# Heads' stage of a spectral attention kernel: (key, head) chunks, one transfer for each repeated block, head weights written once

## The chip, the cores and the metric

The kernel runs on one core of one Trainium2 chip. The metric is the device time of one execution in microseconds (us), taken as the median of several runs. TensorE is called PE here, its weight load PEld, VectorE DVE, ScalarE ACT, GpSimd POOL and SyncE SP. SP computes nothing in this kernel; it issues most of the DMA transfers, and ACT issues some.

## What is computed

The input is (4, 48, 48, 128). Two layers follow each other, each as x = x + layer(group norm of x).

- Layer 0 is a state-space scan in four directions over 2304 positions, with a depthwise convolution ahead of it and a gate after it. The change does not touch it.
- Layer 1 takes each image as 48 tokens (the index that the kernel calls t), each a 48 x 128 field. Keys, queries and values of 32 heads are spectral convolutions of the normalized field. Attention between tokens is computed per head, the heads' outputs are projected by another spectral convolution, and two more spectral layers follow.

The core of layer 1 in the reference:

```
scores = einsum('bhtd,bhsd->bhts', q, k) / sqrt(d)
attn_w = softmax(scores, axis=-1)
out    = einsum('bhts,bhsd->bhtd', attn_w, v)
projd  = fno_layer(out over the 32 heads, wP, wPs, bPs)
```

In the Fourier domain, value and projection weights act mode by mode, so the kernel multiplies them together beforehand. What remains in the heads' stage is a sum over heads h and keys s, for each image b and each mode n:

```
z[b, t, n] = sum over h, s of  attn[b, h, t, s] * G[h, n] * X[b, s, n]
```

G are the head weights (complex, 1536 modes) and X is the spectrum of the tokens. The complex product is formed from three real ones: real parts, imaginary parts, and the sums of both.

## The kernel before

The program is one long list of instructions for five engines. Layer 0 fixes its order by hand. The part of layer 1 up to the end of the heads' stage does not: there a planner orders the instructions of each engine when the program is built, by when operands and buffers come free, and it puts in the waits. Each engine then runs its own list strictly in order. This holds for SP and ACT as issuers of transfers too: an issue whose buffer is still in use holds up all the issues behind it. `dmas` is the pair SP queue, ACT queue; the other transfers here are on SP.

**Head weights (L750 to L794).** The product G is formed in gw as 12 blocks of 128 modes. For each of four blocks k of 384 modes, PE transposes it to [32 heads, 3 x 384] (pgt), ACT copies it to gtt, and SP writes it to the scratch tensor dgt in HBM. dgt has an axis of 16 between the head and the modes: each head's row is written 16 times over, so that a later load of 8 heads fills 128 partitions from 128 rows.

**The stretch after it (L950 to L1030).** `spectral_weights` makes 16 blocks of weights for the later layers: POOL multiplies (wih), PE multiplies (psw, with three PSUM buffers in its pool), ACT copies to spw (L979, one buffer), SP writes spw to sp_d (L980). Beside it stand the group norm of xa, the first instance norm (`first_norm`: pm_in, then pv_in on PE, result in_r), and the forward transform along the width (`forward_w`: pa_x on PE, a_x on DVE, written to da_x), whose result comes back transposed as a2. The loads of the query and key weights (w_wQ, w_wK, many small transfers) are on SP's queue too.

**Scores (L1085 to L1170).** For each of two pairs of images the scores (sc) of all heads are accumulated on PE. DVE and ACT compute the softmax for eight heads at a time: maximum, exponential, sum, and the product sn with the reciprocal sum. Three transposes (pat) put 128 rows on the partitions: a chunk is one group g of 8 heads and one group q of 16 keys, and row 16 * head + key of it is one (head, key). ACT copies the result to attn_c. Beside this, `keys` writes the token spectrum to the scratch tensor dxt, rows of 3 x 384 numbers per token.

**Ahead of the heads' loop (L1190 to L1220).** wpv takes the products of two weight vectors per head, spread over the rows of a chunk; mask marks for each row which key it is. Both come in by eight small transfers per tensor, one for each run of 16 partitions. DVE forms e_w from them, and PE multiplies it with attn_c (pa, 48 matmuls for each pair), which ACT copies to a0_bd.

**The heads' loop (L1221 to L1275).** It runs over 2 pairs x 4 blocks of modes (8 blocks). One block takes three groups q of 16 keys and four groups g of 8 heads, 12 units:

- x (xrep, two buffers) holds, for both images, the 16 keys of group q repeated for 8 heads, on 128 partitions. It comes in as 8 transfers per image.
- r (grep, four buffers) holds the head weights of group g, each head repeated for 16 keys. It is loaded at q = 0 and kept for the block.
- ACT copies two thirds of r to gp in PSUM (two buffers); DVE multiplies gp with x into v; POOL multiplies the last third of r with x into v3. Both results have two buffers.
- PE contracts v and v3 with attn_c into acc, three PSUM banks with one buffer each, over the 12 units.

At the end of a block ACT copies the first bank to s1, DVE combines the three into zt (three instructions), PE transposes zt twice (pz), and ACT copies each to z2.

Of the kernel before, what the change touches and what calls it, by code (L numbers as in the profile page):

```python
# [10 lines left out]
F32 = mybir.dt.float32  # L11
# [8 lines left out]
B, T, H, W = 4, 48, 48, 128  # L20
# [9 lines left out]
NH = 32  # L30
# [613 lines left out]
def layer1(ctx, tc, io, x1_dram, out):  # L644
# [5 lines left out]
    nc = tc.nc  # L650
# [3 lines left out]
    dram = ctx.enter_context(tc.tile_pool(name="l1_dram", bufs=1, space=DRAM))  # L654
    dmas = [nc.sync, nc.scalar]
# [9 lines left out]
    ident = load("ident1", [128, 128], io["c_ident"])  # L665
# [84 lines left out]
    ws_p = everywhere("ws_p", io["wPs"].rearrange("o h -> (o h)"), NH)  # L750

    NC = 384
    dgt = dram.tile([4, NH, 16, 3 * NC], F32, name="dgt")
    with ExitStack() as pw:
        ps_t = pw.enter_context(tc.tile_pool(name="l1_wt", bufs=2, space=PSUM))
        q1 = pw.enter_context(tc.tile_pool(name="l1_w1", bufs=1))

        w_p = q1.tile([128, 12, 2, NH], F32, name="w_p")
        w_v = q1.tile([128, 6, 2, NH], F32, name="w_v")
        d48 = [q1.tile([128, 128], F32, name=f"d48{c}") for c in range(2)]  # L760
        for c in range(2):
            dmas[c].dma_start(w_p[:, :, c], io["wP"][c].rearrange("(j p) h -> p j h", p=128))
            dmas[c].dma_start(w_v[:, :, c], io["wV"][c].rearrange("(j p) h -> p j h", p=128))
            dmas[c].dma_start(d48[c], io[("c_D48r", "c_D48i")[c]])
        for c in range(2):
            p = ps_t.tile([128, 512], F32, tag="tr", name=f"pv48{c}")
            nc.tensor.matmul(p[:, 0:NH], d48[c], w_v[:, 0, c], start=True, stop=True)
            nc.scalar.copy(w_v[:, 0, c], p[:, 0:NH])
        gw = q1.tile([128, 12, 3, NH], F32, name="gw")
        for c in range(2):  # L770
            nc.vector.tensor_mul(gw[:, :, c], w_p[:, :, c], ws_v[:, None, :].to_broadcast([128, 12, NH]))
        half = [128, 6, NH]
        for c in range(2):
            g6 = gw[:, 0:6, c]
            t1 = q1.tile(half, F32, tag="gt", name=f"gt{c}_0")
            nc.vector.tensor_mul(t1, w_v[:, :, c], ws_p[:, None, :].to_broadcast(half))
            nc.vector.tensor_add(g6, g6, t1)
            for i in range(2):

                t2 = q1.tile(half, F32, tag="gt", name=f"gt{c}_{i + 1}")  # L780
                nc.vector.tensor_mul(t2, w_p[:, 0:6, i], w_v[:, :, (c + i) % 2])
                (nc.vector.tensor_sub if c == 0 and i == 1 else nc.vector.tensor_add)(g6, g6, t2)
        nc.vector.tensor_add(gw[:, :, 2], gw[:, :, 0], gw[:, :, 1])

        for k in range(4):
            gt = q1.tile([NH, 3, NC], F32, name=f"gtt{k}")
            for c in range(3):
                p = ps_t.tile([128, 512], F32, tag="tr", name=f"pgt{k}_{c}")
                for j in range(3):
                    nc.tensor.transpose(p[0:NH, j * 128 : (j + 1) * 128], gw[:, 3 * k + j, c], ident)  # L790
                nc.scalar.copy(gt[:, c], p[0:NH, 0:NC])
            nc.sync.dma_start(
                dgt[k], gt.rearrange("h c n -> h (c n)")[:, None].to_broadcast([NH, 16, 3 * NC])
            )  # L794
    ws_q = everywhere("ws_q", io["wQs"].rearrange("h o -> (h o)"), NH)
    ws_k = everywhere("ws_k", io["wKs"].rearrange("h o -> (h o)"), NH)
    a0_bd = const.tile([96, 2, 96], F32, name="a0_bd")
# [6 lines left out]
    dxt = dram.tile([B, 4, T, 3 * NC], F32, name="dxt")  # L804
# [272 lines left out]
    with ExitStack() as ph:  # L1077
# [33 lines left out]
        for pair in range(2):  # L1111
            sc = ps_1.tile([128, 4, 512], F32, tag="sc", name=f"sc{pair}")
            for jn in range(12):
                j, n = divmod(jn, 3)
                shape = [128, NH, T]
                on_pool = jn % 3 == 2
                f = []
                for b in range(2):
                    f.append(pf.tile(shape, F32, tag="f", name=f"f{pair}_{jn}_{b}"))
                    (nc.gpsimd if on_pool else nc.vector).tensor_mul(  # L1120
                        f[b],
                        (g_qk if on_pool else gp)[:, n, j, :, None].to_broadcast(shape),
                        ks[:, j, n, 2 * pair + b, None].to_broadcast(shape),
                    )
                for g in range(4):
                    for b in range(2):
                        nc.tensor.matmul(  # L1127
                            sc[64 * b : 64 * b + 64, g, 0 : 8 * T],
                            qs[:, j, n, 2 * pair + b],
                            f[b][:, 8 * g : 8 * g + 8],  # L1130
                            start=(jn == 0),
                            stop=False,
                        )
                for _ in range(2 - jn % 2 if pair == 0 else 1 + jn % 2):
                    next(beside, None)
            for g in range(4):
                for b in range(2):
                    nc.tensor.matmul(
                        sc[64 * b : 64 * b + T, g, 0 : 8 * T],
                        s0[:, 2 * pair + b],  # L1140
                        d_qk[:, 8 * g : 8 * g + 8],
                        start=False,
                        stop=True,
                    )
            for g in range(4):
                t = f"{pair}_{g}"
                v = sc[:, g, 0 : 8 * T].rearrange("p (h s) -> p h s", s=T)
                shape = [128, 8, T]
                mx = p2.tile([128, 8], F32, tag="mx", name=f"mx{t}")
                nc.vector.tensor_reduce(mx, v, AX.X, ALU.max)  # L1150
                s = p2.tile(shape, F32, tag="s", name=f"s{t}")
                nc.vector.tensor_sub(s, v, mx[:, :, None].to_broadcast(shape))
                nc.scalar.activation(s, s, AF.Exp, scale=scale)
                sm = p2.tile([128, 8], F32, tag="sm", name=f"sm{t}")
                nc.vector.tensor_reduce(sm, s, AX.X, ALU.add)
                nc.vector.reciprocal(sm, sm)
                sn = p2.tile([128, 3, 8, 16], F32, tag="sn", name=f"sn{t}")
                nc.vector.tensor_mul(
                    sn.rearrange("t q h r -> t h q r"),
                    s.rearrange("t h (q r) -> t h q r", r=16),  # L1160
                    sm[:, :, None, None].to_broadcast([128, 8, 3, 16]),
                )
                p = pst.tile([128, 512], F32, tag="tr", name=f"pat{t}")
                for q in range(3):
                    nc.tensor.transpose(
                        p[:, q * 128 : (q + 1) * 128], sn[:, q].rearrange("t h r -> t (h r)"), ident
                    )
                nc.scalar.copy(
                    attn_c[:, 2 * pair : 2 * pair + 2, g],
                    p[:, 0:384].rearrange("p (q b t) -> p b q t", b=2, t=64),  # L1170
                )
# [9 lines left out]
    with ExitStack() as ph:  # L1181
# [7 lines left out]

        wpv = p1.tile([128, 2, 4], F32, name="wpv")  # L1190
        mask = p1.tile([128, 3, T], F32, name="mask")
        for i in range(8):
            rows = slice(i * 16, i * 16 + 16)
            for c, n in enumerate(("wPs", "wVs")):
                w = io[n].rearrange("a b -> (a b)").rearrange("(g i) -> i g", i=8)
                dmas[c].dma_start(wpv[rows, c], w[i].partition_broadcast(16))
            nc.sync.dma_start(mask[rows], io["c_ident"][0:T, 0:T].rearrange("(q r) s -> r q s", r=16))
        nc.vector.tensor_mul(wpv[:, 0], wpv[:, 0], wpv[:, 1])
        e_w = []
        for g in range(4):  # L1200
# [19 lines left out]
        for pair in range(2):  # L1220
            for k in range(4):  # L1221
                acc = [ps_y.tile([128, 512], F32, tag=f"acc{c}", name=f"acc{pair}_{k}_{c}") for c in range(3)]
                gr = []
                for q in range(3):
                    x = p2.tile([128, 2, 3, NC], F32, tag="xrep", name=f"xrep{pair}_{k}_{q}")
                    for b in range(2):
                        for i in range(8):
                            nc.sync.dma_start(  # L1228
                                x[16 * i : 16 * i + 16, b].rearrange("p c n -> p (c n)"),
                                dxt[2 * pair + b, k, q * 16 : q * 16 + 16],  # L1230
                            )
                    for g in range(4):
                        t = f"{pair}_{k}_{q}_{g}"
                        if q == 0:
                            r = pg.tile([128, 3, NC], F32, tag="grep", name=f"grep{t}")
                            nc.sync.dma_start(
                                r.rearrange("p c n -> p (c n)"),
                                dgt[k, 8 * g : 8 * g + 8].rearrange("h r n -> (h r) n"),
                            )
                            gr.append(r)  # L1240
                        r = gr[g]
# [591 lines left out]
```

## Time and profile before

The median of three runs is 5074.72 us (5069.09 to 5077.64). Times of single instructions come from one profiled execution; the numbers in the middle column are where the stage begins and ends in it.

| What | From, to (us) | us |
|---|---|---|
| profiled execution, as timed | | 5081.34 |
| its span in the trace | 0, 5079.4 | 5079.4 |
| heads' loop, first to last accumulation matmul | 4543.8, 4808.8 | 265 |
| all DMA traffic over the span | | 509.25 MB, mean 100 GB/s |

Over the whole span PE is busy 4207.3 us, DVE 4169.1, POOL 4034.6 and ACT 2923.0. These sums are dominated by layer 0, so they say little about the stages that follow it. There one reads the queues and the waits in the stretch itself. A timeline line gives start, length, engine, line of the program, operation, output <- inputs, shapes, how many instructions were merged, and in brackets the idle time before it and what ended it. A line of the busy table gives a stretch of time, its length, the busy time of PE, PEld, DVE, ACT and POOL with the number of instructions, then the clock that PE was granted (1.00 is full), the mean busy share of the 16 DMA engines and the GB/s that they moved.

### The profile page before, as it was taken

The page shows a single profiled execution, that of the slowest core. Times are in us where ns is not written, and L with a number is a line of the kernel's source. Part 1 is how long each engine was busy: PE and PEld are TensorE (multiplying, and loading weights), DVE is VectorE, ACT ScalarE, POOL GpSimd, SP SyncE. Part 2 cuts the span into 40 slices and gives each one's busy share as a digit, 9 for nine tenths or more (in the row PEclk, how much of TensorE's full clock was granted, in tenths as well). Part 3 has the DMA queues.
Part 4 walks back from the last instruction along what each step waited for, and adds up shares of the span by engine and source line. Part 5 has one row for each costly group of instructions (what it writes and reads, how often), then busy time and mean ns, then how long its engine had stood idle before and what let it go on. Part 6 is the DMA issues. An engine that isn't in the chain of part 4 may idle for free. (4 is left out here: it accounts for less than half of the span.)

```text
span 5079.4 us, 44364 instructions
## 1 busy us (share of the span) xinstructions
PE 4207.3 (83%) x12344; PEld 1893.5 (37%) x12344; DVE 4169.1 (82%) x2888; ACT 2923.0 (58%) x6467; POOL 4034.6 (79%) x2219
## 2 busy tenths in 40 slices
PE   6889898888798988887989888878787785888876
PEld 2334333333343333333433333333333332453343
DVE  3689998989899989898999898999999873356636
ACT  3566566666565666665656666656666652223334
POOL 4589998988899989888999898999999873246532
PEclk9989999999899999998999999999999987889977
DMA  1223232322233323222333232333332216236646
GB/s 54 73 88 101 92 114 92 101 88 98 94 106 105 106 91 101 88 98 94 106 103 107 91 102 88 97 105 106 100 103 92 97 66 131 59 82 171 162 106 153
DMA packets 276766, 509.25 MB, mean 100 GB/s; under 512 B 100602, under 2 KB 185434, under 8 KB 276326
## 3 DMA queue, kind: packets, MB, share of 16 engines
q1 hardware_dynamic: 265318, 502.61, 32.5%
q10 hardware_dynamic: 11200, 3.81, 0.5%
q8 instruction: 97, 1.59, 0.1%
q14 instruction: 151, 1.24, 0.1%
HBM read 462.58 MB, written 43.72 MB: 100 GB/s over the span
## 5 line engine op out<-in xcount | busy, mean ns | idle before, releaser
L50 POOL TENSOR_TENSOR hc<-h,cbc 128x960 f32<-128x960 f32 (+1 forms) x1280 | 2719.7, 2140 | 449.2 <-DVE h L50 338.4
L50 DVE TENSOR_TENSOR_SCAN h<-da,carry,db 128x961 f32<-128x961 f32 (+1 forms) x1280 | 2702.4, 2129 | 153.8 <-ACT carry L50 106.0
L50 ACT ACTIVATE da<-dt,a_neg 128x480 f32<-128x480 f32 (+1 forms) x2560 | 1661.3, 649 | 1233.9 <-DVE h L50 1189.3
L50 PE MATMUL yp<-hc,ident 128*128 128x480 f32 (+1 forms) x5120 | 2273.9, 572 | 6.6 <-POOL hc L50 6.4
L50 PEld LDWEIGHTS yp<-hc,ident 128*128 128x128 f32 x5120 | 1006.3, 198 | 1409.7 <-issue 1018.9
L50 DVE TENSOR_TENSOR db<-du,pb 128x960 f32<-128x960 f32 (+1 forms) x960 | 1063.8, 1108 | 232.2 <-PE pb L50 176.8
L50 POOL TENSOR_TENSOR db<-du,bbc 128x960 f32<-128x960 f32 (+1 forms) x320 | 688.6, 2152 | 0.0
L50 PE MATMUL pb<-bs,pick 112*128 112x480 bf16 (+1 forms) x960 | 359.2, 374 | 391.3 <-DVE db L50 389.9
L50 PE MATMUL pc<-pad,cdiag 128*128 128x480 f32 (+1 forms) x630 | 284.6, 564 | 9.0 <-ACT pad L50 9.0
L1249 POOL TENSOR_TENSOR v<-grep,xrep 128x768 f32<-128x768 f32 x96 | 174.1, 1820 | 115.9 <-PE acc L1253 57.7
L1253 PE MATMUL acc<-v,attn_c 128*64 128x384 f32 x1152 | 214.8, 514 | 28.0 <-POOL v L1249 17.8
L1245 DVE TENSOR_TENSOR v<-gp,xrep 128x1536 f32<-128x1536 f32 x96 | 165.1, 1754 | 86.8 <-DMA xrep<-dxt 35.2
L50 POOL TENSOR_TENSOR du<-dt,xc 128x480 f32<-128x480 f32 (+1 forms) x160 | 205.0, 1282 | 37.2 <-ACT dt L50 37.2
L50 ACT COPY db<-carry 128x1 f32<-128x1 f32 x1280 | 226.7, 177 | 7.5 <-DVE db L50 4.2
L50 PE MATMUL px<-xc,w_xp 128*112 128x480 f32 (+1 forms) x320 | 215.0, 759 | 17.0 <-ACT xc L50 13.3
L50 PEld LDWEIGHTS <-pick 112*128 112x128 bf16 x960 | 97.9, 102 | 335.4 <-issue 311.8
L50 ACT ACT_TABLE_LOAD x147 | 188.6, 1283 | 25.7 <-PE gv_g L50 13.8
L50 PE MATMUL pd<-xd,w_dt 8*128 8x480 f32 (+1 forms) x320 | 167.6, 604 | 39.3 <-ACT bs L50 24.4
L50 ACT COPY carry<-h 128x2 f32<-128x2 f32 x1024 | 193.2, 189 | 0.0
L50 PEld LDWEIGHTS pc<-pad,cdiag 128*128 128x128 f32 x630 | 122.1, 195 | 142.4 <-issue 114.7
L50 PE MATMUL yp<-y,ident 128*128 128x480 f32 (+1 forms) x240 | 164.6, 815 | 0.2
L1253 PEld LDWEIGHTS acc<-v,attn_c 128*64 128x64 f32 x1152 | 89.8, 142 | 149.2 <-issue 65.8
(366 smaller groups left out, 3128.9 us busy)
## 6 DMA issues: line engine op xcount, KB each, us to landing
cbc<-cd SPq DMA_DIRECT2D x512, 480.0 KB
bbc<-cd SPq DMA_DIRECT2D x256, 240.0 KB
cbc<-cd SPq DMA_DIRECT2D x128, 384.0 KB
xrep<-dxt SPq DMA_DIRECT2D x384, 72.0 KB
grep<-dgt SPq DMA_DIRECT2D x32, 576.0 KB
bbc<-cd SPq DMA_DIRECT2D x64, 192.0 KB
dgt<-gtt SPq DMA_DIRECT2D x4, 2304.0 KB
x<-in_xT SPq DMA_DIRECT2D x16, 288.0 KB
```

The source lines that it names most:

```text
L50: return lambda *args, **kw: self._tc.keep_in_program_order(emit(*args, **kw))
L1245: nc.vector.tensor_mul(v, gp[:, None, :, 0:NC].to_broadcast([128, 2, 2, NC]), x[:, :, 0:2])
L1249: nc.gpsimd.tensor_mul(v3, r[:, 2:3].to_broadcast([128, 2, NC]), x[:, :, 2])
L1253: nc.tensor.matmul(acc[c][64 * b : 64 * b + 64, 0:NC], attn_c[:, 2 * pair + b, g, q], v[:, b, c] if c < 2 else v3[:, b], start=first, stop ...
```

## The change

Four edits, all in layer 1:

1. dgt loses its axis of 16: each head's row is written once.
2. A chunk's rows lie as (key, head), row 8 * key + head in place of 16 * head + key. sn is laid out as [3, 16, 8], and the product that fills it writes with a step of 8 elements; the transposes read contiguous rows as before.
3. x comes in as one transfer per image. Its source repeats each of 16 rows 8 times by a step of 0. grep reads 8 rows of dgt, and the step of 0 (16 times) is the outermost axis.
4. wpv comes in by four transfers per vector and mask by three, spread over both queues, in place of eight each. wpv's transfers put 8 heads on the partitions 16 times over.

```
-    dgt = dram.tile([4, NH, 16, 3 * NC], F32, name="dgt")
+    dgt = dram.tile([4, NH, 3 * NC], F32, name="dgt")
...
-            nc.sync.dma_start(
-                dgt[k], gt.rearrange("h c n -> h (c n)")[:, None].to_broadcast([NH, 16, 3 * NC])
-            )
+            nc.sync.dma_start(dgt[k], gt.rearrange("h c n -> h (c n)"))
...
-                sn = p2.tile([128, 3, 8, 16], F32, tag="sn", name=f"sn{t}")
+                sn = p2.tile([128, 3, 16, 8], F32, tag="sn", name=f"sn{t}")
                 nc.vector.tensor_mul(
-                    sn.rearrange("t q h r -> t h q r"),
+                    sn.rearrange("t q r h -> t h q r"),
...
-                        p[:, q * 128 : (q + 1) * 128], sn[:, q].rearrange("t h r -> t (h r)"), ident
+                        p[:, q * 128 : (q + 1) * 128], sn[:, q].rearrange("t r h -> t (r h)"), ident
...
-        for i in range(8):
-            rows = slice(i * 16, i * 16 + 16)
-            for c, n in enumerate(("wPs", "wVs")):
-                w = io[n].rearrange("a b -> (a b)").rearrange("(g i) -> i g", i=8)
-                dmas[c].dma_start(wpv[rows, c], w[i].partition_broadcast(16))
-            nc.sync.dma_start(mask[rows], io["c_ident"][0:T, 0:T].rearrange("(q r) s -> r q s", r=16))
+        for c, n in enumerate(("wPs", "wVs")):
+            w = io[n].rearrange("a b -> (a b)")
+            for g in range(4):
+                dmas[c].dma_start(wpv[:, c, g : g + 1], w[8 * g : 8 * g + 8][None].to_broadcast([16, 8]))
+        for q in range(3):
+            dmas[q % 2].dma_start(
+                mask[:, q], io["c_ident"][16 * q : 16 * q + 16, 0:T][:, None].to_broadcast([16, 8, T])
+            )
...
-                        for i in range(8):
-                            nc.sync.dma_start(
-                                x[16 * i : 16 * i + 16, b].rearrange("p c n -> p (c n)"),
-                                dxt[2 * pair + b, k, q * 16 : q * 16 + 16],
-                            )
+                        nc.sync.dma_start(
+                            x[:, b].rearrange("p c n -> p (c n)"),
+                            dxt[2 * pair + b, k, q * 16 : q * 16 + 16][:, None].to_broadcast([16, 8, 3 * NC]),
+                        )
...
-                                dgt[k, 8 * g : 8 * g + 8].rearrange("h r n -> (h r) n"),
+                                dgt[k, 8 * g : 8 * g + 8][None].to_broadcast([16, 8, 3 * NC]),
```

## The prediction

> **What bounds the kernel now.** I read the page first, then the SP queue, the copies on ACT and the busy shares around the place where the head weights are written, then PE and the chain of waits in the heads' stage. On the page PE is busy 83% of the span, DVE 82%, POOL 79%; but until about 4190 us that is the scan of layer 0, which the diff doesn't touch. Its four places lie after it. The transfers concerned, from the page:
>
> ```profile
> xrep<-dxt SPq DMA_DIRECT2D x384, 72.0 KB
> grep<-dgt SPq DMA_DIRECT2D x32, 576.0 KB
> ...
> dgt<-gtt SPq DMA_DIRECT2D x4, 2304.0 KB
> ```
>
> So 9.4 MB is written for head weights of 0.6 MB, and each row block of x comes in 16 pieces. First the writing. Busy shares of two stretches of 10 us (the last two numbers are the DMA engines' share and GB/s), then the SP queue (start, length, what it issued), then ACT:
>
> ```profile
> 4250.00:4260.00 10.00, 1.52 (x4) 1.13 (x5) 6.53 (x10) 1.55 (x2) 0.03 (x1) 0.67 0.98 200
> 4260.00:4270.00 10.00, 10.00 (x27) 5.53 (x27) 0.00 (x0) 0.00 (x0) 0.00 (x0) 0.82 0.98 200
> ```
>
> ```profile
> 4235.38 9.02 SPq L792 DMA_DIRECT2D dgt<-gtt  x4
> 4244.49 12.52 SPq L980 DMA_DIRECT2D sp_d<-spw  x1
> 4257.06 11.39 SPq L894 DMA_DIRECT2D w_wK<-in_wK  x5
> 4303.29 0.33 SPq L980 DMA_DIRECT2D sp_d<-spw  x1
> ```
>
> ```profile
> 4242.41 0.48 ACT L979 COPY spw<-psw 96x384 f32<-96x384 f32 x1
> ...
> 4302.79 0.48 ACT L979 COPY spw<-psw 96x384 f32<-96x384 f32 x1
> 4305.26 0.47 ACT L979 COPY spw<-psw 96x384 f32<-96x384 f32 x1 [1.99 <-DMA sp_d<-spw]
> ```
>
> The dgt write fills the DMA engines until 4284 (9.4 MB at 200 GB/s is 47 us). Right behind it on SP's queue stands the first of 16 sp_d writes, and spw has one buffer, so the second spw copy can't come before that write has landed. It runs 60 us after the first, behind the whole first norm. The other steps then follow at 2.46 us each (copy, write, wait), and PE reaches the forward transform (pa_x) only at 4332.92, although in_r, the norm's last result, was ready at 4302.1. Those 30.8 us lie on the chain of waits.
>
> Second the heads' loop. The chain of waits around one x block, then PE over the same block of 12 units:
>
> ```profile
> 4688.28 1.83 POOL v L1249
> 4690.12 0.30 SPq L1228
> ...
> 4696.95 3.03 DMA xrep<-dxt
> ```
>
> ```profile
> 4713.40 1.50 PE L1253 MATMUL acc<-v,attn_c 128*64 128x384 f32 x6
> 4716.53 1.51 PE L1253 MATMUL acc<-v,attn_c 128*64 128x384 f32 x8 [1.63 <-DVE v L1245]
> 4718.20 14.28 PE L1253 MATMUL acc<-v,attn_c 128*64 128x384 f32 x82 [0.15 <-DVE v L1245]
> 4734.58 9.86 PE L1253 MATMUL acc<-v,attn_c 128*64 128x384 f32 x48 [2.11 <-POOL v L1249]
> ```
>
> POOL frees the x buffer at 4690.12, SP needs until 4697.4 for 16 issues, and the last lands at 4699.98: 9.9 us. PE runs a third (48 matmuls) in 8.18 us [...], so x is late. The line with 2.11 is that wait; it recurs about once per block.
>
> Third the prologue. One line of DVE:
>
> ```profile
> 4527.03 0.16 DVE L1198 TENSOR_TENSOR wpv<-wpv 128x4 f32<-128x4 f32 x1 [2.82 <-DMA mask<-in_c_ident]
> ```
>
> PE's pa waits for what follows from it and begins at 4527.76, while its other operand, attn_c, is complete at 4525.75 (the last ACT copy starts at 4525.27 and takes 0.48).
>
> [...] in 4000 to 4127, where layer 0 loads mostly cbc (each row spread over 128 partitions), 91 GB/s move at a share of 0.27, or 337 at a full share. [...] here 16 issues cost 7.3 us against about 2 to land. [...] Here 48 matmuls take 8.18 us after waits of 1.59 to 1.79, and 9.71 to 9.86 after waits of 2.11 to 2.41[...].
>
> **The change part by part.** The profiled execution took 5081.3 us (span 5079.4), 6.6 over the median 5074.7; I make the sum on the profile and take it from the median.
>
> Head weights. The four writes shrink to 144 KB each, 0.6 MB or 3 us at 200 GB/s; the four issues on SP stay. The first sp_d lands about 2 us after its issue, so spw's second copy can be planned at about 4247 and the chain of 2.46 us steps runs beside the norm. I expect the planner to do so, because the present order shows it ordering by readiness: four steps' psw run early (three psum buffers and one copy), then nothing until the write would be through. Twelve steps are left, 4 matmuls or 1.50 us of PE each, 18 us. PE idles beside the norm for 8.0 us (4250.9 to 4258.9), 4.1 (4276.9 to 4281.0) and 3.1 (4299.1 to 4302.2). At a step per 2.46 us about four fit; eight may push pm_in and pv_in back, 8 x 1.5 = 12 us. Gain 30.8 if all hides, 30.8 - 12 = 18.8 if none of the eight does; I take 22. The w_wK loads, which SP holds until after 4303, come forward too. POOL's wih (0.82 each, 1.65 per step) fits where POOL waited 27.7 us before 4277. Next late is pa_x with its DVE evictions and then the a2 load of 12.6 us, both unchanged.
>
> x in one transfer per image. Issues per third fall from 16 to 2 (0.42 each, from the chain). 1.18 MB at about 300 GB/s (the windows of 2 us over greps show 306 to 401) is 3.9 us, and a small write's round trip of 1.86 less its data 0.5 is 1.4: together 6.1 us against 9.9. Two buffers give it four units of PE, 12 x 0.174 = 2.09 each, 8.4 us, so it lands 2.3 us early. At a block's turn four greps (0.6 MB, 2 us each) stand in the same queue ahead of x for the second third, which then has the turn besides: 8 + 6 against 8 + 8.4, enough. PE is late next. A block without the waits is turn 7.97 (4710.23 to 4718.20) + 14.28 + 8.18 = 30.43. The zt groups, at 4571.17 first and 4808.80 last, give a mean of 33.95 for seven blocks: 7 x 3.52 = 24.6. The first block loses its 1.74. Together 26.3.
>
> grep. The same bytes, read from 8 rows 16 times over instead of from 128 rows. No trace shows just this; cbc's single row bounds it at no loss. The bound on the other side is the rival below.
>
> wpv and mask. 24 issues become 11, SP from 16 to 6, ACT from 8 to 5 (0.42 median), so they land before attn_c: pa starts at 4525.8, a gain of 1.9. It can't be more, since softmax sets the rest. On ACT, exponentials stand behind such issues (a wait of 2.04 at 4520.3), fewer now.
>
> (key, head) order. DVE's sn write steps 8 elements instead of 1. It takes 0.55 us for 384 elements; bounds 0 and twice that, at most 8 x 0.55 = 4.4, of which the second pair's 2.2 lies open. I take 0. The transposes and attn_c keep their shapes.
>
> Sum 22 + 26.3 + 1.9 = 50 us: 5025.
>
> **Rivals.**
> (a) The turns shorten too. Now the gp copies of the next block stand behind both z copies on ACT, and v starts 4.5 us after the last accumulation. With grep issued up to 8 us sooner the planner may put gp ahead. PE could then start after pz: 3.2 + 96 x 0.174 = 19.9 against 7.97 + 14.28 = 22.25, or 2.35 x 7 = 16 us: 5009. For it: two gp copies run before the loop already, since their greps were early. Against: ACT's order is fixed at build and I can't read it.
> (b) The sp_d chain stays behind the norm, or pushes the norm back as much as it gains: 28 us remain, 5047. For it: PE and ACT are in order, and a psw placed too early blocks pm_in.
> (c) Slower: many engines reading the same few rows at once halve the rate. x and grep are 28.3 + 18.9 = 47.2 MB. At 145 GB/s that is 325 us against the present loop of 272, +53, less 24 gained elsewhere: +29, 5104. It decides below 47.2 MB / (272 + 24) = 159 GB/s. Against it: cbc.
> (d) No effect: all transfers were covered. The 2 us waits and the 30.8 us speak against it.
>
> **How the numbers follow.** Forecast 0.47 (5010 to 5037), (a) 0.25, (b) 0.16, (c) 0.09, (d) 0.03. The measurement can't tell 0.2%, 10 us, from no change. Faster is forecast, (a) and nearly all of (b), 0.86; same is (d) and the edge of (b), 0.05; slower is (c), 0.09. The range reaches from 4998, (a) with the full 30.8 of the first part, to 5056, (b) with a slow sn and a third of the loop's gain missing.
>
> **What would show it.** The DMA share near zero from 4250 to 4285; spw copies between 4247 and 4290; pa_x starting at about 4311; no xrep wait in front of POOL's v, and runs of 48 matmuls at 8.18 back to back; zt groups 30.4 us apart (28 for (a), over 36 for (c)). I am wrong if spw's second copy still follows in_r, or if the heads' stage shows a DMA share near 1 at under 200 GB/s.

## The result and the profile after

| | median, us | runs |
|---|---|---|
| before | 5075.88 (5069.09 to 5079.39) | 7 |
| after | 5055.04 (5052.61 to 5060.62) | 7 |
| ratio | 0.9962, 95% interval 0.9950 to 0.9973 | |

The change gains 20.8 us of the 50 forecast. The profiled execution of after took 5055.04 us, its span is 5053.3. The two profiles lie further apart than the medians, by 26.1 us of span, and 4.2 of this is layer 0. Cut at the end of layer 0 (the last product with po, written to ws), the last score (sc), the first matmul into acc and the last zt, the two spans stand so:

| stretch, us | before | after | difference | forecast |
|---|---|---|---|---|
| layer 0, to the last product with po | 4196.0 | 4191.8 | -4.2 | 0 |
| setup: to the last score | 319.5 | 291.6 | -27.9 | -22 |
| prologue: to the first acc | 28.3 | 32.9 | +4.6 | -1.9 |
| heads' loop: to the last zt | 266.8 | 266.4 | -0.4 | -26.3 |
| the rest | 268.8 | 270.6 | +1.8 | 0 |

The first row is the same program twice, so it shows how far two executions differ; the differences in it and in the last row are not explained by anything below. The loop is where the forecast fell: most of the waits for x are gone, and the loop is as long as before.

The transfers do what the diff says. From the page of after:

```profile
xrep<-dxt SPq DMA_DIRECT2D x48, 576.0 KB
grep<-dgt SPq DMA_DIRECT2D x32, 576.0 KB
```

**Setup.** SP's queue of after (start, length, what it issued), then ACT's copies of spw:

```profile
4232.26 4.34 SPq L792 DMA_DIRECT2D dgt<-gtt  x4
...
4239.07 0.30 SPq L978 DMA_DIRECT2D sp_d<-spw  x1
...
4242.25 0.33 SPq L978 DMA_DIRECT2D sp_d<-spw  x1
```

```profile
4238.57 0.47 ACT L977 COPY spw<-psw 96x384 f32<-96x384 f32 x1
4241.75 0.47 ACT L977 COPY spw<-psw 96x384 f32<-96x384 f32 x1 [2.29 <-PE psw L975]
...
4296.28 0.46 ACT L977 COPY spw<-psw 96x384 f32<-96x384 f32 x1
```

The second copy comes 3.2 us after the first instead of 60.4, and all sixteen are through by 4296.7, beside the norm. From 4250 to 4285 the DMA engines' share is 0.12 to 0.24. The forward transform (pa_x) now runs almost without a stop from 4313.20, 121.4 us after layer 0's end in place of 136.9 (after, then before, where it still waited for a copy of spw):

```profile
4313.20 9.65 PE L730 MATMUL pa_x<-xa,fw 128*66 128x384 f32 x24
```

```profile
4332.92 0.86 PE L730 MATMUL pa_x<-xa,fw 128*66 128x384 f32 x2 [0.85 <-ACT spw L979]
```

**Prologue.** DVE of after, the product of wpv and the first e_w:

```profile
4495.77 0.16 DVE L1198 TENSOR_TENSOR wpv<-wpv 128x4 f32<-128x4 f32 x1 [4.18 <-DMA mask<-in_c_ident]
...
4499.23 0.36 DVE L1203 TENSOR_SCALAR e_w<-mask,wpv 128x144 f32<-128x144 f32 x1 [2.14 <-DMA mask<-in_c_ident]
```

mask lands later after the scores than before, though there are fewer transfers: the wpv product comes 12.4 us after the last score (4483.4), before it was 11.5 (4527.03 after 4515.5), and e_w then waits 2.14 us more for mask. The chain of waits has the last mask transfer, from issue to landing (after, then before), and a busy line of after shows what the DMA engines do meanwhile:

```profile
4490.23 8.78 DMA mask<-in_c_ident
```

```profile
4525.21 1.68 DMA mask<-in_c_ident
```

```profile
4489.00:4490.00 1.00, 0.80 (x3) 0.40 (x3) 1.00 (x2) 0.48 (x2) 0.00 (x0) 0.50 0.05 0
```

The issue comes earlier than before, 6.8 us after the last score in place of 9.7; the landing takes 7.1 us longer. A share of 0.05 at 0 GB/s is no load by bytes. But wpv is 1024 numbers of 4 bytes in either kernel (2 vectors, 4 groups, 128 rows), and the DMA records of the traces show them going one by one, about 120 in a us in after and 130 in before, so some 8 us in both. That mask waits behind these pieces is read from the order of the records and was not tried apart.

**Heads' loop.** Waits of before (4570 to 4811) and of after (4540 to 4790): engine and line, what it waited for, us in total, times, longest:

```profile
DVE v L1245 <- DMA xrep<-dxt: 32.9, 12, 3.5
...
POOL v L1249 <- DMA xrep<-dxt: 18.8, 10, 3.0
POOL v L1249 <- DMA grep<-dgt: 5.8, 2, 3.1
```

```profile
ACT gp L1242 <- DMA grep<-dgt: 73.7, 26, 7.1
...
PE acc L1252 <- ACT s L1260: 30.2, 7, 5.3
...
POOL v L1248 <- DMA grep<-dgt: 19.4, 12, 3.4
...
DVE v L1244 <- DMA xrep<-dxt: 4.2, 5, 2.2
```

DVE's waits for x fell from 32.9 us to 4.2. In their place ACT waits for grep, and PE waits 30.2 us, seven times, once per turn of a block, for s1, ACT's copy of the old block's accumulator: acc has one buffer, so no new block starts before s1 is copied. The chain of waits over one turn of after (start, length, what) shows how these join; behind it PE over the same turn:

```profile
4568.23 8.03 DMA grep<-dgt
...
4576.34 0.81 ACT gp L1242
...
4577.17 1.77 DVE v L1244
4578.94 0.80 ACT gp L1242
4579.74 0.42 ACT s L1260
```

```profile
4568.16 7.96 PE L1252 MATMUL acc<-v,attn_c 128*64 128x384 f32 x48 [0.16 <-DVE v L1244]
4580.20 1.53 PE L1252 MATMUL acc<-v,attn_c 128*64 128x384 f32 x4 [4.08 <-ACT s L1260]
4582.45 2.82 PE L1252 MATMUL acc<-v,attn_c 128*64 128x384 f32 x4 [0.73 <-DVE v L1244]
...
4588.00 14.40 PE L1252 MATMUL acc<-v,attn_c 128*64 128x384 f32 x84
```

The old block ends at 4576.12. ACT could copy s1 then, but two gp copies of the next block stand ahead of it, and s1 begins only at about 4579.7. The first of the two waits for a grep that was issued at 4568.23 and landed after 8.03 us; 1.18 MB of x, issued just before, were under way ahead of it. In the kernel before, s1 and both z copies stood ahead of gp. After the wait four matmuls take 2.82 us, at a granted clock of 0.5.

Windows of 2 us at a turn (the last two numbers are the DMA engines' share and GB/s), in before while greps load, in after likewise:

```profile
4602.00:4604.00 2.00, 2.00 (x16) 1.21 (x13) 1.87 (x2) 0.00 (x0) 1.39 (x2) 1.00 0.91 336
4604.00:4606.00 2.00, 2.00 (x15) 1.16 (x12) 0.26 (x1) 0.34 (x1) 1.89 (x2) 1.00 1.01 376
```

```profile
4606.00:4608.00 2.00, 2.00 (x14) 0.86 (x12) 1.82 (x2) 0.22 (x1) 1.82 (x1) 1.00 1.05 240
4608.00:4610.00 2.00, 2.00 (x16) 0.91 (x14) 1.10 (x1) 0.00 (x0) 1.82 (x1) 1.00 1.00 233
```

The engines are as busy, but move 233 to 240 GB/s instead of 336 to 376. A grep of 0.59 MB so takes 2.5 us and not 1.6 to 1.75, x of both images 5.0 and not 3.9. The experiments ask why, and whether this is what holds the loop.

Where the loop's time went can be reckoned from PE's 1152 matmuls into acc. Call the turn, as the prediction does, the time from the end of an old block to the fifteenth matmul of the new one (4576.12 to 4588.00 above, 11.88 us), and the rest the other 130 matmuls of the block. Means of the seven blocks that follow a turn, in us:

| | turn | rest of the block |
|---|---|---|
| before | 8.17 | 25.78 |
| forecast | 7.97 | 22.46 |
| after | 12.09 | 22.06 |

So inside the blocks the gain came as forecast, 7 x 3.72 = 26.0 us, and the turns took it back, 7 x 3.92 = 27.4.

### The profile page after: what moved, and what is told of

It is laid out like the page before. It is cut to its first block, busy times and chain, and to the rows that moved or that the text cites. A ratio compares the mean times of both kernels' runs of the same rounds, so it can differ in the third digit from the quotient of the medians.

```text
span 5053.3 us, 43909 instructions
## 1 busy us (share of the span) xinstructions
PE 4188.2 (83%) x12344; PEld 1911.3 (38%) x12344; DVE 4174.2 (83%) x2888; ACT 2921.3 (58%) x6467; POOL 4036.1 (80%) x2219
## 3 DMA queue, kind: packets, MB, share of 16 engines
q1 hardware_dynamic: 257734, 493.72, 33.1%
## 5 line engine op out<-in xcount | busy, mean ns | idle before, releaser
L1252 PE MATMUL acc<-v,attn_c 128*64 128x384 f32 x1152 | 218.9, 513 | 36.1 <-ACT s L1260 30.2
L50 PE MATMUL px<-xc,w_xp 128*112 128x480 f32 (+1 forms) x320 | 213.9, 756 | 16.9 <-ACT xc L50 13.3
L50 PE MATMUL pd<-xd,w_dt 8*128 8x480 f32 (+1 forms) x320 | 167.9, 605 | 39.8 <-ACT bs L50 24.7
L1242 ACT COPY gp<-grep 128x768 f32<-128x768 f32 x96 | 77.0, 803 | 158.0 <-DVE v L1244 84.3
```

The lines of the kernel that those rows point to most:

```text
L50: return lambda *args, **kw: self._tc.keep_in_program_order(emit(*args, **kw))
L1242: nc.scalar.copy(gp[:, :, 0:NC], r[:, 0:2])
L1252: nc.tensor.matmul(acc[c][64 * b : 64 * b + 64, 0:NC], attn_c[:, 2 * pair + b, g, q], v[:, b, c] if c < 2 else v3[:, b], start=first, stop ...
```

## The experiments

Lengths of the stretches, each from one profile, and the medians. Each group of runs had its own runs of before: 5068.07 for order by hand, copies and loops exchanged, 5072.42 for short transfers early, flat greps, and exchanged and early, 5072.24 for the last three. The ratios are to these. The one kernel that was profiled twice (exchanged and early) had loops of 242.2 and 243.2 us, so differences of about 1 us are not interpreted.

| kernel | setup | prologue | loop | median, us | ratio to before |
|---|---|---|---|---|---|
| before | 319.5 | 28.3 | 266.8 | 5075.88 | |
| after | 291.6 | 32.9 | 266.4 | 5055.04 | 0.9962 |
| ACT's order by hand | 295.8 | 32.9 | 307.7 | 5099.51 | 1.0060 (1.0046 to 1.0073) |
| copies of dgt, same form | 316.5 | 32.6 | 265.8 | 5082.01 | 1.0025 (1.0014 to 1.0035) |
| loops exchanged | 292.4 | 33.0 | 241.7 | 5035.90 | 0.9937 (0.9924 to 0.9951) |
| short transfers early | 292.4 | 25.2 | 266.5 | 5051.06 | 0.9956 (0.9944 to 0.9968) |
| flat greps | 353.8 | 32.6 | 248.7 | 5094.95 | 1.0041 (1.0028 to 1.0054) |
| exchanged and early | 288.2 | 25.5 | 242.2 | 5025.54 | 0.9911 (0.9898 to 0.9924) |
| dxt written twice | 289.8 | 58.9 | 266.3 | 5082.02 | 1.0019 (1.0010 to 1.0028) |
| exchanged, early, fifth buffer | 292.3 | 25.1 | 231.7 | 5014.25 | 0.9890 (0.9875 to 0.9905) |
| the same, dxt written twice | 289.8 | 53.0 | 234.4 | 5038.42 | 0.9931 (0.9918 to 0.9943) |

**The rates by themselves.** A kernel with loads alone; nothing of the model is computed. Two of its ways to fill a tile:

```
sp.dma_start(t[:, j], rows[16 * j : 16 * j + 16][:, None].to_broadcast([16, 8, 1152]))
sp.dma_start(t[:, j], rows[0:512].rearrange("(r h) n -> r h n", h=32)[:, 8 * j : 8 * j + 8])
```

> Nothing of the model is computed here: ten ways to load four pieces of 128 rows each, one way after the other, with a full wait between. Theory R (reading the same rows many times is slow): 128 different rows of 4608 B, also with the axis of 16 given a real stride, come at 330 to 400 GB/s; 8 rows read 16 times, 16 rows read 8 times and one row read 128 times at about 230. Rival F (the form of the address, three axes, is what costs, not the repeats): the strided form without repeats is at 230 as well, and one row over 128 partitions is fast. Rival L (long rows are what costs, since layer 0 moves repeated rows of 1920 B at over 300): eight rows of 480 numbers, repeated, are fast, and rows of 1152 and 1024 slow. 16 partitions in 8 pieces: 285, as in the kernel before.

Four transfers of 590 KB on the three axes of x, each row read 8 times, took 12.93 us from the first issue to the sum behind them. The same axes with 128 different rows took 12.81, one row on 128 partitions 9.48. So the repeats don't cost here, at rows of 4608 B (12.93 us with, 12.81 without); the form does. With rows of 1920 B the form shows little: 16 by 8 with repeats (g) took 5.96 us, 128 rows on two axes 5.53; the transfers landed 3.7 and 3.3 us after their issue in the median.

```profile
150.87 2.15 DVE L89 TENSOR_REDUCE sums<-g 128x1 f32<-128x1920 f32 x1 [5.96 <-DMA g<-in_xT]
158.55 2.15 DVE L89 TENSOR_REDUCE sums<-h_480d 128x1 f32<-128x1920 f32 x1 [5.53 <-DMA h_480d<-in_xT]
```

So rival L is right in part: of the row lengths tried, the form was slow with the long rows only. Where between 1920 and 4096 B this begins was not tried (16 by 8 with rows of 4096 B took 11.66 us for 2.1 MB). The first two ways ran while stores of zeros were still under way and are not used; the later run of the rates has them undisturbed.

**ACT's order by hand.** gp, s1 and z in the loop are issued in the order in which they are written, so s1 and z stand ahead of the next block's gp.

```
+        on = Ordered(tc)
...
-                        nc.scalar.copy(gp[:, :, 0:NC], r[:, 0:2])
+                        on.scalar.copy(gp[:, :, 0:NC], r[:, 0:2])
...
-                nc.scalar.copy(s1, acc[0][:, 0:NC])
+                on.scalar.copy(s1, acc[0][:, 0:NC])
...
-                    nc.scalar.copy(
+                    on.scalar.copy(
```

> The kernel after, with the copies on ACT in the heads' loop kept in the order of the program, so that s1 and both z copies stand ahead of the next block's gp. Theory O (gp was placed ahead of s1, and waits for grep, which now arrives late): the 30 us of PE waiting for s1 are gone, blocks fall from 34.1 to about 30.5 us, the loop from 264 to about 240, the whole to about 5031. Rival D (the loop is bound by the transfers themselves, whatever the order): 5.9 MB per block at 228 GB/s are 26 us and pile up at the turns, so the wait only moves from s1 to v, blocks stay at 33 to 34 and the whole within 8 us of 5055.

Slower, and the loop 41 us longer than in after, which neither theory has. The planner put SP's loads in another order too (the first grep of a block ahead of that block's first x, the other three behind it), so the run doesn't isolate ACT's order. Its waits from 4525 to 4832:

```profile
POOL v L1249 <- DMA xrep<-dxt: 48.1, 16, 4.0
PE acc L1253 <- POOL v L1249: 46.2, 31, 2.9
```

The wait for s1 went, and one for x by way of POOL came. The DMA engines are full through the turn (a share of 0.99 to 1.11 from 4584 to 4602), and another late transfer took its place; how much of the 41 us is SP's order was not tried.

**Copies of dgt, same form.** dgt holds sixteen copies again, and grep reads 128 different rows, on the same three axes as in after.

```
-    dgt = dram.tile([4, NH, 3 * NC], F32, name="dgt")
+    dgt = dram.tile([4, 16, NH, 3 * NC], F32, name="dgt")
...
-                                dgt[k, 8 * g : 8 * g + 8][None].to_broadcast([16, 8, 3 * NC]),
+                                dgt[k, :, 8 * g : 8 * g + 8],
```

> The kernel after, with the head weights again written 16 times over, so that grep reads 128 different rows (with the same three axes). This undoes the first part of the change and the repeated reads of grep; x stays as after. Setup: the first norm and the sp_d chain are one behind the other again, so the scores end about 28 us later than after. Loop: theory R expects grep to land in time (at over 330 GB/s), gp ahead of s1 then costs nothing, and blocks fall to 28 to 30.5 us, the loop by 25 to 40 us; rival F expects blocks of 34 us as in the kernel after. Whole: about 5050 by R, 5083 by F.

The loop stays at 265.8 us, as rival F has it, and at a turn (4600 to 4614) the windows show 228 to 251 GB/s without any repeated row in grep. The setup goes back to 316.5. So the one writing of dgt is worth some 25 us (316.5 less 291.6), and reading rows many times over costs nothing that this shows (a loop of 266.4 us with repeats in grep, 265.8 without).

**Loops exchanged.** k outside, the pair of images inside; each k's greps are loaded once for both pairs.

```
-        for pair in range(2):
-            for k in range(4):
+        for k in range(4):
+            for pair in range(2):
...
-                gr = []
+                gr = gr if pair else []
...
-                        if q == 0:
+                        if q == 0 and pair == 0:
```

> The kernel after, with the loop over the mode blocks outside and the pair inside, so that each block's grep is loaded once and serves both pairs: 16 loads in place of 32, and four of the seven turns have none. Theory O: the four turns without grep lose the wait of about 4.3 us for s1 and are short (block about 28.5), the three others stay at 34.1; loop 264 to about 242, whole about 5033. Rival D, transfers as such: 3.5 MB per block in place of 5.9 in half of the blocks, also faster, but then the three turns with grep shorten too, since x is less behind. If neither holds (the turn's length is set by zt, pz and z), the whole stays within 8 us of 5055.

The loop falls by 24.7 us. PE's waits for s1 are left at the three turns that load new greps:

```profile
PE acc L1252 <- ACT s L1260: 13.5, 3, 5.2
```

The forms, and the order of gp ahead of s1, are as in after. The three turns with new greps take 12.71 us in the mean, about as in after (12.09); the four without take 5.53, less than the 8.17 of before. So the loop of after is held by the greps at its turns. That the loop, 241.7, comes near the forecast's 240.5 is chance, since no turn has the length that the forecast gave it.

**The rates again, more ways.** Loads alone, as above, with stores only at the end.

> Nothing of the model is computed: twelve ways of filling a tile of 128 partitions, four transfers of 590 KB each (1.18 MB for three of them), one way at a time with a sum on VectorE between, and no stores until the end. Time from the first issue to the sum's start. Theory F[...]: 128 rows on two axes, whether all different (a), one row (e) or at a pitch of two rows (f), 8.5 to 9.5 us; the three-axis forms, repeated inside (c), outside (b) or not at all (d), 12 to 13.5; c on two issuing queues (g) the same as c; the 1.18 MB transfer of 128 rows (h) 15 to 17; eight pieces of 16 rows to 16 neighbouring partitions (i) 30 or more, the same pieces to every eighth partition (j) at most 20; c as two transfers to every second partition (k) between c and a; 32 rows each four times (l) slower than or like c. Theory R (repeated rows read one place of DRAM): b, c, e, g, k and l slow, a, d, f fast. Theory Q (one issuing queue is the limit): g faster than c by a quarter or more.

DVE's sums, in order; the number in brackets is DVE's idle time before the sum, which begins within 0.2 us of the first issue:

```profile
8.83 4.95 DVE L91 TENSOR_REDUCE sums<-a_distinct 128x1 f32<-128x4608 f32 x1 [7.96 <-DMA a_distinct<-in_xT]
26.37 4.95 DVE L91 TENSOR_REDUCE sums<-b_eight 128x1 f32<-128x4608 f32 x1 [12.59 <-DMA b_eight<-in_xT]
43.74 4.95 DVE L91 TENSOR_REDUCE sums<-c_sixteen 128x1 f32<-128x4608 f32 x1 [12.43 <-DMA c_sixteen<-in_xT]
61.76 4.95 DVE L91 TENSOR_REDUCE sums<-d_strided 128x1 f32<-128x4608 f32 x1 [13.06 <-DMA d_strided<-in_xT]
76.24 4.95 DVE L91 TENSOR_REDUCE sums<-e_one 128x1 f32<-128x4608 f32 x1 [9.53 <-DMA e_one<-in_xT]
...
106.35 4.95 DVE L91 TENSOR_REDUCE sums<-g_queues 128x1 f32<-128x4608 f32 x1 [11.87 <-DMA g_queues<-in_xT]
...
173.07 9.75 DVE L91 TENSOR_REDUCE sums<-i_block 128x1 f32<-128x9216 f32 x1 [38.40 <-DMA i_block<-in_xT]
206.88 9.75 DVE L91 TENSOR_REDUCE sums<-j_step 128x1 f32<-128x9216 f32 x1 [24.06 <-DMA j_step<-in_xT]
...
242.48 4.95 DVE L91 TENSOR_REDUCE sums<-l_thirty 128x1 f32<-128x4608 f32 x1 [9.10 <-DMA l_thirty<-in_xT]
```

Windows from the middle of a, b, c and l (DMA share and GB/s last):

```profile
4.00:6.00 2.00, 0.00 (x0) 0.00 (x0) 1.00 1.04 408
18.00:24.00 6.00, 0.00 (x0) 0.00 (x0) 1.00 1.02 236
36.00:42.00 6.00, 0.00 (x0) 0.00 (x0) 1.00 1.00 241
...
236.00:241.00 5.00, 0.00 (x0) 0.00 (x0) 1.00 1.00 359
```

At a full share, 128 rows on two axes move 408 GB/s, x's and grep's new forms 236 to 241, with or without repeats (d, without, 238). A second issuing queue changes little (11.87 us against 12.43 for c), and so do two transfers to every second partition (k, 11.79 us). One row 128 times (335 GB/s in the middle) is faster than the forms of 16 or 8 rows here (236 to 262 in theirs) and slower than 128 rows. Three ways missed what was expected of them: j_step took 24 us where at most 20 was expected, four transfers of 128 rows of 9.2 KB took 13.62 us where 15 to 17 was, and the form of 32 rows each read 4 times moves 359 GB/s, where theory F expected it slow.

Windows from the middle of h, i and j, all with rows of 9.2 KB:

```profile
116.00:124.00 8.00, 0.00 (x0) 0.00 (x0) 1.00 1.01 426
145.00:165.00 20.00, 0.00 (x0) 0.00 (x0) 1.00 1.04 132
190.00:200.00 10.00, 0.00 (x0) 0.00 (x0) 1.00 1.02 218
```

So 128 rows (h) move 426 GB/s, pieces of 16 rows to 16 neighbouring partitions (i) 132, the same pieces to every eighth partition (j) 218. No trace shows which engine wrote which partition. So the forms' rates are shown, and their cause is not.

**Short transfers early.** wpv, mask and wpv's product stand before the scores.

```
+    wpv = pm.tile([128, 2, 4], F32, name="wpv")
+    mask = pm.tile([128, 3, T], F32, name="mask")
...
-        wpv = p1.tile([128, 2, 4], F32, name="wpv")
-        mask = p1.tile([128, 3, T], F32, name="mask")
```

> The transfers of wpv and mask, and wpv's product, stand before the scores instead of behind them; all else as in the kernel after. Theory P (what the prologue lost is that these short transfers land about 10 us after the scores' end and the first products of attn_c wait for them): the time from the last score to the first acc falls from 32.9 us to 26 to 28.5, and the kernel takes 5049 to 5050, 5 to 6 us less than after. Rival N (the prologue is bound by the first x and grep, which are queued behind the short transfers and land then): they go ahead by the time of the issues alone, about 2 us, and the kernel takes 5053. Rival S (the short transfers push back the spectral weights in the setup, whose chain sets the scores' end): 5055 or more.

The prologue falls from 32.9 to 25.2 us; theory P had expected 26 to 28.5. So the late short transfers were the prologue's loss, and more than that: 25.2 is also less than the 28.3 of before. The median lies 4 us under after's, but in another group of runs, and the two intervals of the ratio overlap: the stretch shows the gain, the kernel's time alone would not.

**Flat greps.** x as in after, but grep in the form of the kernel before, one transfer of 128 neighbouring rows, in the new order of partitions.

```
-    dgt = dram.tile([4, NH, 3 * NC], F32, name="dgt")
+    dgt = dram.tile([4, 4, 16, 8, 3 * NC], F32, name="dgt")
...
-            nc.sync.dma_start(dgt[k], gt.rearrange("h c n -> h (c n)"))
+            for g in range(4):
...
-                                dgt[k, 8 * g : 8 * g + 8][None].to_broadcast([16, 8, 3 * NC]),
+                                dgt[k, g].rearrange("r h n -> (r h) n"),
```

> dgt is written sixteen times over again, but so that each grep is one transfer of 128 neighbouring rows on two axes; partitions, consumers and x's transfers are as in the kernel after. Theory F: each grep takes 1.5 to 2 us of full share instead of 2.6, so a turn's burst of x, four greps and x falls from 20.8 us to about 18, a turn is 1.5 to 2.5 us shorter, and the heads' loop takes 248 to 254 us instead of 264.5. Rival D (the DRAM or the engines give about 225 GB/s at this place whatever the form, since x's transfers run at the same time): the loop stays at 262 to 266 us. In both the setup gives back part of what it gained, as dgt's larger writes stand in the queue: the scores end up to 27 us later, as in the run with the copies, if the planner moves the chain of the spectral weights back, and not if it doesn't; the loop's own length decides.

A window at a turn, while greps load, and PE's waits for s1 in the loop (4582 to 4830):

```profile
4608.00:4610.00 2.00, 0.00 (x0) 0.00 (x0) 1.41 (x1) 1.37 (x3) 2.00 (x2) 1.00 1.02 408
```

```profile
PE acc L1256 <- ACT s L1264: 16.5, 7, 3.0
```

The greps run at 408 GB/s, the seven waits are 16.5 us in place of 30.2, and the loop is 248.7 us, as theory F expected. The turn falls to 9.86 us in the mean, and the rest of the block, 21.79, hardly changes. This splits the loop's nothing into two terms: with grep's old form the change would gain 18.1 us of loop (266.8 less 248.7), and grep's new form costs 17.7 of it again. The setup is 62 us longer than after's, where at most 27 was expected: the sixteen writes of dgt, each from 8 partitions, occupy SP's queue until 4306.0. That side wasn't followed further.

**Exchanged and early.**

> The loops over k and pairs are exchanged and each k's greps are loaded once for both pairs, and the short transfers stand before the scores. If the two gains add: loop 240 us as in the run with the exchange alone, prologue 26 to 28.5, kernel 5028 to 5032. If the prologue's gain is taken back by the first turn (the first x and grep then stand in the same burst): 5035.

The gains add: loop 242.2, prologue 25.5, 5025.54 us. Repeated on another occasion:

> A repeat of the loops exchanged with the short transfers early: 5022 to 5030 on this chip's terms, loop 242 us.

5023.35 us (5021.01 to 5025.68), loop 243.2.

**dxt written twice.** The test of the fast form for x: 32 rows, each read 4 times.

```
-    dxt = dram.tile([B, 4, T, 3 * NC], F32, name="dxt")
+    dxt = dram.tile([B, 4, T, 2, 3 * NC], F32, name="dxt")
...
-                            dxt[2 * pair + b, k, q * 16 : q * 16 + 16][:, None].to_broadcast([16, 8, 3 * NC]),
+                            dxt[2 * pair + b, k, q * 16 : q * 16 + 16]
+                            .rearrange("t d n -> (t d) n")[:, None]
+                            .to_broadcast([32, 4, 3 * NC]),
```

> Each row of dxt is written twice, so that x's transfer has a first axis of 32 rows, each read four times, instead of 16 read eight times; the same bytes reach the same partitions, and grep's form is as in the kernel after. Theory A (the first axis of a transfer sets its rate: 16 rows give about 190 to 240 GB/s, 32 or 128 give 260 to 300, as in the run of the rates): x of both images takes about 4.5 us of full share in place of 5.2 to 6.2, a turn's burst is 1.5 to 3 us shorter, and the heads' loop takes 250 to 257 us instead of 266.4. Rival C ([...] repeats by four stay slow in the loop): 264 to 268. The doubled writes of dxt (3.5 MB more) lie beside the scores; if they don't, the scores end later by up to 15 us, whichever holds.

A window in which x of a next block loads, and the waits of the loop (4540 to 4830):

```profile
4596.00:4598.00 2.00, 2.00 (x15) 1.52 (x13) 1.82 (x2) 0.85 (x2) 1.84 (x2) 1.00 0.98 380
```

```profile
ACT gp L1246 <- DMA grep<-dgt: 75.5, 28, 7.2
...
PE acc L1256 <- ACT s L1264: 27.7, 7, 5.8
```

x runs at 380 GB/s, more than the 260 to 300 of theory A, yet the loop stays at 266.3, which theory A did not expect. Rival C has the number but not the reason, since the repeats by four were fast. The waits for grep and s1 are nearly those of after, and so is the turn (12.34 us). At a turn ACT's gp copies at 4638.50, 4641.04, 4643.52 and 4646.08 each wait for their grep, 2.5 to 2.6 us apart, and SP needs 6.32 us from 4629.85 for the four issues, beside three v of POOL of 1.8 us each. From this it is read that the turn ends with the greps, whose buffers POOL frees only in the old block's last units, and that x ahead of them is covered. So it is grep's rate, not x's, that took the gain. The doubled writes of dxt, for which xt has one buffer, also put off the first x: before the loop ACT waits 63.8 us for them (36.0 in after), and DVE then 41.1 us for x (9.0 in after); the prologue is 26 us longer.

**A fifth buffer for grep,** with the exchange and the early loads, so that the first new grep doesn't wait for an old one's last read.

```
-        pg = ph.enter_context(tc.tile_pool(name="l1_qg", bufs=4))
+        pg = ph.enter_context(tc.tile_pool(name="l1_qg", bufs=5))
```

> As the loops exchanged with the short transfers early, with a fifth buffer for grep, so that the first grep of the next k can land before the turn. If the turn waits for the first grep alone, the three turns with new greps lose about 4 us each, loop 229 to 234 us, kernel 5014 to 5018. If the second to fourth grep, which still wait for the last reads of the old ones, end last, the gain is the time of one grep per turn (2.6 us), loop 234 to 238, kernel 5018 to 5022. If the loads are not moved ahead in SP's queue, nothing: 242 and 5025.

The loop falls to 231.7 us, the kernel to 5014.25, the fastest here. PE's waits for s1 in it (4509 to 4741), which were 13.3 us without the fifth buffer:

```profile
PE acc L1252 <- ACT s L1260: 5.7, 3, 2.7
```

The first of the expected cases is the one measured: loop 229 to 234, kernel 5014 to 5018. The three turns with new greps take 8.69 us in the mean, where they took 12.23 without the fifth buffer.

> Loops exchanged, short transfers early, fifth grep buffer and dxt written twice, all together. If the gains add: loop 226 to 234 us, kernel 5008 to 5018. If x's form doesn't matter once the greps are loaded half as often, the same as with the fifth buffer alone.

With dxt written twice besides, 5038.42 us, which neither of the two cases has: the prologue loses 28 us and the loop wins nothing.

## Why the prediction was off

**Setup, right in its mechanism; its size is in part luck.** What held the stretch (the dgt write in front of sp_d, the single spw buffer) went as said. The norm was put back by 14.6 us, where the prediction allowed up to 12. So pa_x's unbroken run starts 15.5 us sooner, less than the 18.8 given as the low end. What the sum had left out is pa_x itself, "unchanged" in it: six of its 48 matmuls already run in the norm's gaps and the others wait little for DVE, so the stretch from 4313.20 to the end of pa_x at 4329.59 is 16.4 us, against 25.5 before (4332.92 to 4358.46). With that, and some 3 us further on, the setup gains 27.9.

**The loop, wrong, and this is the failed step.** The sum took the turn as unchanged, 7.97 us, with four greps of 2 us loading in it. Of grep's new form it said "cbc's single row bounds it at no loss", and x was taken at "about 300 GB/s (the windows of 2 us over greps show 306 to 401)". Both are rates of transfers of another form: cbc is one row over 128 partitions (335 GB/s in the rates, 337 as the prediction read it), the old greps are 128 rows on two axes. The new forms, 16 by 8, run at 233 to 240 GB/s at a turn, alone at 236 to 241. A grep so takes 2.5 us. With x of the next block ahead of them and more x behind, a turn's burst is 1.18 + 2.36 + 1.18 MB, 20 us at 235 GB/s. The first gp copies wait for it on ACT, s1 waits behind gp, and PE waits for s1: the turn took 12.09 us, and grep's form alone accounts for 17.7 us of loop (after against flat greps).

The x term came in full, 26.0 us inside the blocks, though its rate was wrong too. At 5.0 us instead of 3.9, x would land 7.2 us after its buffer came free, by an estimate with the prediction's other terms, and this is still under the 8.4 that the two buffers give. The margin covered the error.

Flat greps don't bring the turn back to its old length: 9.86 us against 8.17, or 7 x 1.69 = 11.8 us. There gp still stands ahead of s1, and x still has its slow form; how the 11.8 us divide between these was not measured.

Of the prediction's signs, the zt groups lie 33.1 us apart, between the 30.4 of the forecast and the 36 of (c). The heads' stage does show a DMA share near 1, but at 233 to 240 GB/s, above the 200 that it set as the limit.

**Rival (a) saw the order, and its worth shows where no grep is late.** gp does stand ahead on ACT, as (a) has it, and ahead of s1 as well. At the turns without new greps (loops exchanged) the turn is 5.53 us, and (a)'s sum gives 7.97 less 2.35, or 5.62. In after every turn has new greps, they come late, and the same order makes PE wait. Fixing the order by hand moved other queues and made the loop longer, so what the order costs at those turns stays open.

**Rival (c) had the right place for a loss and the wrong cause.** Repeated rows are not slow (c and d of the second rates, with and without, took 12.43 and 13.06 us, within 5%); 16 runs of 8 partitions are, at rows of 4608 B (236 to 241 GB/s against 408 for 128 rows), with repeats or without. The loss is smaller than its 145 GB/s would give, so after is still faster.

**Prologue, wrong in sign.** "24 issues become 11 ... so they land before attn_c" counted issues. The last mask issue did come sooner after the scores (6.8 us in place of 9.7), but it landed 8.78 us later instead of 1.68. The pieces of 4 bytes, which the sum did not count, are as many as before. The run with the loads moved early gives 7.7 us back. Of sn's step of 8 elements, which the sum took at 0, DVE shows 0.85 us in place of 0.56 for each of the eight, 2.3 us in all; half of it lies in this stretch, and it was not tried apart.

## What to carry to other kernels

Take a transfer's rate from one with the same axes on both sides and rows of the same length, not from one with the same bytes. Merging x's small transfers was worth 26 us inside the blocks, but with rows of 4608 B the new form, 16 runs of 8 partitions, moved 236 to 241 GB/s where 128 rows moved 408, 1.7 times the time. Count the pieces of a small transfer as well as its issues (1024 of 4 bytes took some 8 us here). When a stage's loads come in a burst at a turn, ask which one ends last there and when its buffer comes free; loading less at the turn (loops exchanged) and one buffer more gained 35 us of loop where a faster x gained nothing.

## What was not expected of the hardware

- At a full DMA share the same 590 KB, in rows of 4608 B, to 128 partitions move at 408 GB/s (128 rows), 359 (32 rows read 4 times), 335 (one row), 236 to 241 (16 by 8, repeats or not). The share does not tell these rates apart: it is 1.00 to 1.04 in all but the one row's (0.97). With rows of 1920 B the forms of 16 by 8 and of 128 rows lie close, 5.96 and 5.53 us for 1 MB.
- Pieces of 16 rows of 9.2 KB to 16 neighbouring partitions take 38.4 us for 4.7 MB, to every eighth partition 24.1, as four transfers of 128 rows 13.6.
- 1024 numbers of 4 bytes, spread over 128 partitions, take some 8 us at a DMA share of 0.05 to 0.06, in 8 transfers or in 16.
